# A macaron S4 layer on one core: Newton steps moved to VectorE, the S4 tables cut into pieces, the first weight tile copied on chip, and VectorE's instructions kept in program order

## The chip, the core and the metric

The kernel runs on one core of a Trainium2 chip. The core has a matrix engine (TensorE, "PE" in the profile), three engines for element-wise work (VectorE "DVE", ScalarE "ACT", GpSimd "POOL"), and SyncE ("SP"), which here only starts DMA transfers. The engines run side by side and wait for each other with semaphores. Each engine takes its own instructions in the order in which the program was built. The metric is the time of one execution on the device in microseconds (us), as the median of several runs.

## The reference

The input is 2 x 1024 tokens of 1024 numbers. It goes through a gated feed-forward block with 4-bit weights, then an S4 convolution, then the same feed-forward block again, each with a layer norm before it and a residual around it:

```python
def _dequant(qweight, scales, qzeros, g_idx):
    # W[k,n] = scales[g_idx[k],n] * (w4[k,n] - (z4[g_idx[k],n]+1))
...
xf = x.reshape(-1, x.shape[-1])
h = jax.nn.silu(xf @ Wg) * (xf @ Wu)
out = h @ Wd
...
x = x + 0.5 * _L0_ffn_ref(_layernorm(x, axis=-1), ...)
x = x + _L0_attn_ref(_layernorm(x, axis=-1), ...)
x = x + 0.5 * _L0_ffn_ref(_layernorm(x, axis=-1), ...)
```

`Wg` and `Wu` are 1024 x 2752, `Wd` is 2752 x 1024. Scales and zero points are given for groups of 128 rows, so there are 8 groups for gate and up and 21 for down. The S4 kernel is built from 64 complex poles at 1024 roots of unity, turned into a time response by an inverse DFT, and applied to each channel as a causal convolution, which the kernel does as a product with a Toeplitz matrix.

## The kernel before

**Jobs.** The 2048 tokens are four blocks of 512. `JOBS` (L1046) lists eight feed-forward passes: block 0 and block 1 for the first block of the layer, then both for the second, then the same for blocks 2 and 3. In the text they are job 0 to job 7. Each job is `gate_up` (L485) and then `down` (L548).

**gate_up.** The output columns are 21.5 gate columns and 21.5 up columns of 128 ("units"; even units are gate, odd units are up). They are done in eight waves: five of six units, two of four, one of five. A wave is eight steps, one for each weight group, so a job has 64 steps. In a step every unit gets two matmuls of 128 x 512 (the low and the high part of the split input, `xTl` and `xTh`), accumulated in a PSUM bank of its own. After each step but the last the bank is multiplied by the ratio of two scales (`scaled`, L478), so that one bank can sum over groups. Even units are multiplied on ScalarE (L481) and odd units on VectorE (L483); in job 0 one odd unit of each step goes to ScalarE as well. A unit's next matmul waits for its multiplication. At the end of a wave `gated` (L523) takes Silu on ScalarE (L525), the product `hf` on VectorE (L528), and a split into `hh` and `hl` on GpSimd (L530, L532). There are six accumulator banks, two `hf` buffers and six weight buffers (pool `w`).

**down.** 2 x 22 steps of four banks each, scaled in the same way, with weights `wd`. `back` (L580) turns the result and adds it to the residual on VectorE (L587).

**Weights.** In job 0 the 4-bit weights are unpacked: `split` (L395) makes bytes of nibbles, `dequantize` (L400) subtracts zero points (`q`, L404, on VectorE, into a `w` buffer) and writes the tile to DRAM (L406), from where `load_w` (L462) reads it, three steps ahead. Eight `q` tiles make one wave; `first_weights` (L445) places them 12 to 5 steps ahead of their wave. `down` has the same with `qd` (L434).

**Layer norm.** `moments` (L129) runs eight `bn_stats` and four `bn_aggr` and a first guess of the inverse root on VectorE. `deviations` (L150) refines it by three Newton steps of four tiny instructions each on GpSimd (L156 to L159). `normalized` (L163) applies it on VectorE, `turn` (L188) transposes on TensorE and splits into `xTh` (ScalarE) and `xTl` (VectorE). A call stands at one step of the loop: for a job whose predecessor was a first pass, `moments` at steps 4 and 27 (49 in job 1); for a coming first pass, at step 44 (job 0: at the start of `down`).

**S4 tables.** `s4_poles`, `s4_roots`, `s4_response` and `s4_toeplitz` run once, in job 1 at steps 6, 11, 16 and 20. The largest single instruction is a reciprocal of 128 x 1024 (L652). The convolutions of block 0 follow at steps 34 to 46 of job 1.

**Order.** The loops call hooks in program order, but a scheduler orders the instructions of each engine while the program is built, from its own idea of when inputs are ready, so an instruction can be placed ahead of one that was written earlier. The two calls that concern the first tile are

```python
    first = [normalized_on_act(0, t) for t in range(NT)]
    for i in range(8):
        dequantize(0, i)
    for t in range(NT):
        turn(0, t, first[t], 0, acc)
    for t in range(NT):
        turn(0, t, first[t], 1)
```

and before them `warm()` (L199) has 32 transposes of an identity that nothing reads. `in_order` (L317, job 2, step 30) checks on VectorE that group indices and scales are such that the fast path holds.

Of the kernel before, what the change touches and what calls it, by code (L numbers as in the profile page):

```python
# [20 lines left out]
P = 128  # L21
# [28 lines left out]
def macaron_s4_kernel(  # L50
# [31 lines left out]
    nc = tc.nc  # L82
    u = u.flatten_outer_dims()
# [45 lines left out]
    def moments(b, k, first=0, count=NT):  # L129

        ts = range(first, first + count)
        name = f"{b}_{k}_{first}"
        stats = small.tile([P, NT, 2, 6], F32, tag="stats", name=f"stats_{name}")
        mv = small.tile([P, NT, 2], F32, tag="mv", name=f"mv_{name}")
        for t in ts:
            for i in range(2):
                nc.vector.bn_stats(stats[:, t, i, :], x[b][t][:, bass.ts(i, 512)])  # L137
            nc.vector.bn_aggr(mv[:, t, :], stats[:, t, :, :].rearrange("p a s -> p (a s)"))
        own = slice(first, first + count)
        ve = small.tile([P, NT], F32, tag="ve", name=f"ve_{name}")[:, own]  # L140
        nc.vector.tensor_scalar(ve, mv[:, own, 1], EPS, None, ALU.add)
        r = small.tile([P, NT], F32, tag="r", name=f"r_{name}")
        half = small.tile([P, NT], I32, tag="half", name=f"half_{name}")[:, own]
        nc.vector.tensor_scalar(half, ve.bitcast(I32), 1, None, ALU.logical_shift_right)
        nc.vector.tensor_scalar(  # L145
            r[:, own].bitcast(I32), half, -1.0, float(0x5F3759DF), ALU.mult, ALU.add
        )
        ln[b, first] = (mv, ve, r, own)

    def deviations(b, k, first=0, eng=None):  # L150

        eng = eng or nc.gpsimd
        mv, ve, r, own = ln.pop((b, first))
        e = small.tile([P, NT], F32, tag="e", name=f"e_{b}_{k}_{first}")[:, own]
        for _ in range(3):
            eng.tensor_tensor(e, r[:, own], r[:, own], ALU.mult)  # L156
            eng.tensor_tensor(e, e, ve, ALU.mult)
            eng.tensor_scalar(e, e, -0.5, 1.5, ALU.mult, ALU.add)
            eng.tensor_tensor(r[:, own], r[:, own], e, ALU.mult)  # L159
        for t in range(own.start, own.stop):  # L160
            ln[b, t] = (mv[:, t, 0:1], r[:, t : t + 1], k)

    def normalized(b, t):  # L163
# [3 lines left out]
        return n  # L167

    def normalized_on_act(b, t):
        m, r, k = ln[b, t]  # L170
        n = t4(f"xn_{b}_{k}_{t}")
        less = small.tile([P, 1], F32, tag=f"less{t}", name=f"less_{t}")
        nc.gpsimd.tensor_scalar(less, m, -1.0, None, ALU.mult)
        nc.scalar.activation(n, x[b][t], AF.Identity, bias=less)
        nc.scalar.activation(n, n, AF.Copy, scale=r)  # L175
        return n
# [21 lines left out]

    def warm():  # L199

        ps = bank("warm")
        for _ in range(32):
            nc.tensor.transpose(ps[:, :P], ident, ident)
# [53 lines left out]
    def scales(part):  # L257


        lo = HID * part  # L260
        n = min(HID, WIDE * P - lo)
        row = t4(f"srow_{part}")
        for m, src in enumerate((gate_s, up_s)):
            nc.scalar.dma_start(row[m * GK : (m + 1) * GK, :n], src[:, lo : lo + n])
        ps = bank(f"ps_s{part}")
        u0, u1 = 16 * part, 16 * part + 2 * (n // P)
        for k in range(n // P):
# [3 lines left out]
        if u1 == UNITS - 1:  # L271
            row = t2("srow_half")
            for m, src in enumerate((gate_s, up_s)):
                nc.scalar.dma_start(row[:GK, m * HALF : (m + 1) * HALF], src[:, WIDE * P :])
            nc.tensor.transpose(ps[:, bass.ts(2 * (n // P), GK)], row[:GK, :P], ident[:GK, :GK])
# [4 lines left out]
        inv = t2(f"inv_{part}")[:, : (u1 - u0) * GK]  # L280
        inverse(inv, flat(s), part)
# [35 lines left out]
    def in_order():  # L317

        nc.gpsimd.memset(ok, 1.0)
        nc.sync.dma_start(row_t, c_row)  # L320
        nc.sync.dma_start(shift_t, c_shift)
        in_range(s_gu.rearrange("p u g -> p (u g)"), 0)
        in_range(s_dn.rearrange("p c g -> p (c g)"), 2)
        raw = t4("ix").bitcast(I32)[:32, : 3 * P].rearrange("p (i k) -> p i k", i=3)
# [44 lines left out]

    packed = {}  # L370
# [9 lines left out]
    def fetch_zeros(w):  # L380
        z = t4(f"z_{w}").bitcast(BF16)[:, : width_of(w)]
# [859 lines left out]
```

## Time and profile before

| | us |
|---|---|
| median of 3 runs | 2231.79 |
| lowest and highest run | 2229.93, 2232.19 |
| the profiled execution, as timed | 2234.3 |
| its span in the profile | 2232.5 |
| first matmul of job 0 starts at | 35.8 |
| first matmul of job 1 starts at | 321.2 |
| first matmul of job 2 starts at | 634.8 |
| last transposes start at | 2219.3 |

The profile names an instruction by its line, its engine, its output and inputs, and gives busy time and the mean duration of one. "Idle before" is the time that the engine stood still just before an instruction, with what ended it. Matmuls are pipelined: the profile gives each of the 128 x 512 kind 0.39 us, but they start every 0.23 us. The row PEclk is the clock that TensorE was granted, as a share of the full one. A table of windows gives, for each stretch of the span, the busy time and the number of instructions of each engine.

### The profile page before, as it was taken

To read this page: it belongs to the slowest core of one execution; us is meant where nothing else is said; L and a number is where in the kernel's file an instruction comes from. 1 tells how busy PE (TensorE), PEld (TensorE's weight loads), DVE (VectorE), ACT (ScalarE), POOL (GpSimd) and SP (SyncE) were. 2 spreads that over 40 slices of the span, in tenths; PEclk is the share of its full clock that TensorE was granted. 3 is DMA by queue.
4 is the path that set the end of the run, shared out by engine and by line. 5 is a ranking of instruction groups with operands and counts; after the bars stand their busy time and mean duration, and the time that the engine had idled before them with its cause. 6 is when DMAs were issued, how large, how long until landed. Compare 5 with 4: busy or idle time off the path is not lost.

```text
span 2232.5 us, 28079 instructions
## 1 busy us (share of the span) xinstructions
PE 2152.1 (96%) x9396; PEld 1696.8 (76%) x9396; DVE 1693.7 (76%) x2653; ACT 1455.9 (65%) x2235; POOL 361.5 (16%) x496
## 2 busy tenths in 40 slices
PE   5998999999999999999999999999999999999998
PEld 4776677766887777888788878777788777888876
DVE  6887878666786878777877777867778677777776
ACT  4887775535764576677767777646776467767765
POOL 1232003212011230022102220102201023012210
PEclk7999998999999999999999999999999999999999
DMA  6888864324443545744456444435444355564444
GB/s 237 280 280 270 256 216 126 122 86 152 136 147 107 177 137 165 226 144 134 144 174 193 132 137 136 145 107 156 138 136 147 108 176 137 155 188 143 136 134 129
DMA packets 163526, 359.93 MB, mean 161 GB/s; under 512 B 22268, under 2 KB 27429, under 8 KB 163375
## 3 DMA queue, kind: packets, MB, share of 16 engines
q1 hardware_dynamic: 162746, 357.71, 52.2%
q8 instruction: 78, 1.28, 0.2%
q14 instruction: 74, 0.60, 0.1%
q10 hardware_dynamic: 628, 0.34, 0.1%
HBM read 307.25 MB, written 50.73 MB: 160 GB/s over the span
## 4 chain that ended last, share of the span: by engine, by line
PE 53%; issue 31%; POOL 6%; DVE 5%; DMA 3%; ACT 0%; SPq 0%; POOLq 0%; DVEq 0%; ACTq 0%
PE pg L505 28%; PE po L564 18%; PE pc L810 5%; POOL hl L532 3%; POOL hh L530 2%; DVE pg L483 1%; DMA w<-wq 1%; DMA wd<-wdq 1%; PE pt L182 1%; PE pb L585 1%; DVE po L483 1%; PE st L182 1%; DMA wdq<-qd 0%; DVE q L404 0%; DVE hf L528 0%
## 5 line engine op out<-in xcount | busy, mean ns | idle before, releaser
L481 ACT ACTIVATE pg<-pg,rat 128x512 f32<-128x512 f32 x1264 | 825.4, 662 | 475.5 <-PE pg L505 471.9
L505 PE MATMUL pg<-xTl,w 128*128 128x512 f32 x2752 | 1092.5, 398 | 27.0 <-DVE pg L483 16.3
L505 PE MATMUL pg<-xTh,w 128*128 128x512 f32 x2752 | 1077.6, 393 | 0.0
L483 DVE TENSOR_TENSOR pg<-pg,rat 128x512 f32<-128x512 f32 x1144 | 781.5, 696 | 175.7 <-PE pg L505 166.7
L505 PEld LDWEIGHTS pg<-xTl,w 128*128 128x128 f32 x2752 | 521.6, 190 | 163.9 <-DVE pg L483 29.7
L505 PEld LDWEIGHTS pg<-xTh,w 128*128 128x128 f32 x2752 | 522.2, 190 | 104.8 <-issue 0.2
L564 PE MATMUL po<-hl,wd 128*128 128x512 f32 x1344 | 538.7, 403 | 15.4 <-DVE po L483 10.1
L481 ACT ACTIVATE po<-po,ratd 128x512 f32<-128x512 f32 x670 | 437.6, 662 | 169.2 <-PE po L564 168.7
L564 PE MATMUL po<-hh,wd 128*128 128x512 f32 x1344 | 521.7, 392 | 0.0
L483 DVE TENSOR_TENSOR po<-po,ratd 128x512 f32<-128x512 f32 x610 | 418.7, 697 | 92.9 <-PE po L564 88.7
L564 PEld LDWEIGHTS po<-hl,wd 128*128 128x128 f32 x1344 | 252.2, 188 | 94.8 <-DVE po L483 23.7
L530 POOL CAST hh<-hf 128x512 fp32r<-128x512 f32 x168 | 107.8, 642 | 1243.6 <-DVE hf L528 1197.7
L564 PEld LDWEIGHTS po<-hh,wd 128*128 128x128 f32 x1344 | 253.3, 188 | 45.9
L532 POOL TENSOR_TENSOR hl<-hf,hh 128x512 fp32r<-128x512 f32 x168 | 220.9, 1315 | 13.3
L528 DVE SCALAR_TENSOR_TENSOR hf<-pg,rat,g 128x512 f32<-128x512 f32 x168 | 125.3, 748 | 77.7 <-PE pg L505 29.2
L525 ACT ACTIVATE g<-pg,rat 128x512 f32<-128x512 f32 x168 | 115.8, 689 | 41.4 <-PE pg L505 38.5
L810 PE MATMUL pc<-toeplitz,st 128*128 128x512 f32 (+3 forms) x384 | 126.5, 486 | 0.0
L810 PEld LDWEIGHTS pc<-toeplitz,st 128*128 128x128 f32 x384 | 70.3, 190 | 57.3 <-issue 46.0
L156 POOL TENSOR_TENSOR e<-r 128x4 f32<-128x4 f32 x36 | 9.7, 268 | 498.6 <-DVE r L145 496.6
L818 DVE TENSOR_TENSOR x<-x,pc 128x512 f32<-128x512 f32 x32 | 22.0, 687 | 77.6 <-PE pc L810 77.2
L137 DVE BATCH_NORM_STATS2 stats<-x 128x6 f32<-128x512 f32 x96 | 64.8, 680 | 1.4 <-DMA x<-in_L_attn_u_dram 0.2
L182 PE MATMUL pt<-ident,xn 128*128 128x128 f32 x256 | 42.6, 285 | 16.0 <-ACT xn L175 14.1
(136 smaller groups left out, 674.3 us busy)
## 6 DMA issues: line engine op xcount, KB each, us to landing
w<-wq SPq DMA_DIRECT2D x320, 384.0 KB
wd<-wdq SPq DMA_DIRECT2D x336, 256.0 KB
w<-wq SPq DMA_DIRECT2D x128, 256.0 KB
w<-wq SPq DMA_DIRECT2D x64, 320.0 KB
x<-in_L_attn_u_dram SPq DMA_DIRECT2D x32, 512.0 KB
wq<-q SPq DMA_DIRECT2D x40, 384.0 KB
wdq<-qd SPq DMA_DIRECT2D x32, 256.0 KB
xs<-x SPq DMA_DIRECT2D x16, 512.0 KB
```

The lines of the kernel that those rows point to most:

```text
L137: nc.vector.bn_stats(stats[:, t, i, :], x[b][t][:, bass.ts(i, 512)])
L182: nc.tensor.transpose(ps[:, bass.ts(k, P)], n[:, bass.ts(4 * half + k, P)], ident)
L481: nc.scalar.activation(dst, src, AF.Copy, scale=sc)
L483: nc.vector.tensor_tensor(dst, src, sc.to_broadcast([P, TB]), ALU.mult)
L505: nc.tensor.matmul(p, w[:, bass.ts(col, P)], part[:, g, :], start=(g == 0 and k == 0), stop=(g == GK - 1 and k == 1), skip_group_check=True,)
L525: nc.scalar.activation(g, pg, AF.Silu, scale=rat[:, 2 * f, GK - 1 :])
L528: nc.vector.scalar_tensor_tensor(hf, pu, last, g, ALU.mult, ALU.mult)
L530: nc.gpsimd.tensor_copy(hi, hf)
L532: nc.gpsimd.tensor_tensor(lo, hf, hi.bitcast(F32), ALU.subtract)
L564: nc.tensor.matmul(ps[c], w[:, bass.ts(c, P)], part, start=(f == 0 and k == 0), stop=(f == NF - 1), skip_group_check=True,)
L585: nc.tensor.transpose(ps[:, bass.ts(c, P)], yT[a, c][:, bass.ts(t, P)], ident)
L810: nc.tensor.matmul(ps[:, lo - 512 * nh :], lhsT(c), toeplitz[:, lo - P * c : end - P * c], start=(c == 0), stop=(c == last),)
```

## The change

Newton's steps move to VectorE with three instructions each instead of four, and one more that scales the result (constants 3, 12 and 768 and the factor 1/8192 carry the halving). `moments` and `deviations` lose their partial forms. At the start, ScalarE takes the mean off while the moments of the next tile run, the first tile of weights is copied from the `q` buffers into the weight buffer by eight DMAs that ScalarE issues, and the second half of the first block is turned in steps 0 to 3 instead of before step 0. The scales are read in four pieces at steps 2, 12, 20 and 28 instead of three and one (before the loop, 1, 3 and 12), from SyncE's queue. The `q` tiles of wave 1 stand at steps 1 to 4. One of the odd units that ScalarE took in job 0 goes back to VectorE in every fourth step. The S4 functions become one generator, advanced once a step from step 2 of job 1; the reciprocal is cut in eight and two multiplications go to ScalarE; the layer norm, turning and convolution of block 0 in job 1 start eight steps later (the convolutions at steps 42 to 54, `moments` after them at 57). `warm()` is gone. Last, every VectorE instruction is made to follow the one written before it, and so is every ScalarE instruction of the part ahead of the jobs.

```diff
+    def in_written_order(*engines):
+        last = {}
+        for ins in list(nc.cur_bb.bb.instructions):
+            if ins.engine in engines:
+                if ins.engine in last:
+                    tc.add_manual_dep(
+                        ins,
+                        last[ins.engine],
...
+                last[ins.engine] = ins.name
...
-    def deviations(b, k, first=0, eng=None):
-        eng = eng or nc.gpsimd
-        mv, ve, r, own = ln.pop((b, first))
-        e = small.tile([P, NT], F32, tag="e", name=f"e_{b}_{k}_{first}")[:, own]
-        for _ in range(3):
-            eng.tensor_tensor(e, r[:, own], r[:, own], ALU.mult)
-            eng.tensor_tensor(e, e, ve, ALU.mult)
-            eng.tensor_scalar(e, e, -0.5, 1.5, ALU.mult, ALU.add)
-            eng.tensor_tensor(r[:, own], r[:, own], e, ALU.mult)
+    def deviations(b, k, sign=1.0):
+        mv, ve, r = ln.pop(b)
+        e = small.tile([P, NT], F32, tag="e", name=f"e_{b}_{k}")
+        for three in (3.0, 12.0, 768.0):
+            nc.vector.tensor_tensor(e, r, r, ALU.mult)
+            nc.vector.tensor_tensor(e, e, ve, ALU.mult)
+            nc.vector.scalar_tensor_tensor(r, e, three, r, ALU.subtract, ALU.mult)
+        nc.vector.tensor_scalar(r, r, -sign / 8192, None, ALU.mult)
...
+    first_tile = wpool.tile([P, width_of(0)], F32R, tag="w", name="w_0_0")
...
         nc.vector.tensor_tensor(q, src, z, ALU.subtract)
         dst = w_q[w].rearrange("(r j) n -> j r n", j=8)[j]
+        if w == 0:
+            nc.scalar.dma_start(first_tile[j:P:8].bitcast(F32), q[: P // 8].bitcast(F32))
         nc.sync.dma_start(dst, q.bitcast(F32))
...
-                s = s0 + j if w > 1 else j // 2
+                s = s0 + j if w > 1 else (1, 2, 2, 3, 3, 3, 4, 4)[j]
                 at(up, s, lambda w=w, j=j: dequantize(w, j))
...
     def load_w(j, s):
+        if j == s == 0:
+            return first_tile
...
-                    on_act = unit % 2 == 0 or (j == 0 and pos == 1)
+                    on_act = unit % 2 == 0 or (j == 0 and pos == 1 and g % 4 < 3)
...
         dr = t4("s4_dr")
-        nc.vector.tensor_scalar(dr, cs, neg[:, 0:1], None, ALU.mult)
+        nc.scalar.activation(dr, cs, AF.Copy, scale=neg[:, 0:1])
         di = sn
-        nc.vector.tensor_scalar(di, sn, alpha, None, ALU.mult)
+        nc.scalar.activation(di, sn, AF.Copy, scale=alpha)
+        yield
...
-        nc.vector.reciprocal(den, den)
+        for c in range(NC):
+            yield
+            nc.vector.reciprocal(den[:, bass.ts(c, P)], den[:, bass.ts(c, P)])
...
+    def s4_tables():
+        yield from s4_poles()
+        yield
+        yield from s4_roots()
+        yield
+        s4_response()
+        yield
+        s4_toeplitz()
...
-                    late = 22 if j == 1 else 0
+                    late = 30 if j == 1 else 0
...
             if j == 0:
-                at(up, 1, lambda: scales(1))
-                at(up, 3, lambda: scales(2))
-                at(up, 12, scales_down)
+                for s, k0, k1 in ((2, 3, 11), (12, 11, 19), (20, 19, WIDE)):
+                    at(up, s, lambda k0=k0, k1=k1: scales(k0, k1, scale_rows(k0, k1)))
+                at(up, 28, scales_down)
+                for t in range(NT):
+                    at(up, t, lambda t=t: turn(0, t, first[t], 1))
...
             if j == 1:
-                for s, f in ((6, s4_poles), (11, s4_roots), (16, s4_response), (20, s4_toeplitz)):
-                    at(up, s, f)
+                tables = s4_tables()
+                for s in range(2, 42):
+                    at(up, s, lambda: next(tables, None))
...
-    warm()
-    scales(0)
-    split(0)
     fetch_zeros(0)
-    moments(0, 1)
-    deviations(0, 1)
-    first = [normalized_on_act(0, t) for t in range(NT)]
+    srow = scale_rows(0, 3, nc.scalar)
+    first = []
+    def less_mean(t, m):
+        n = t4(f"xn_0_1_{t}")
+        nc.scalar.activation(n, x[0][t], AF.Identity, bias=m, scale=-1.0)
+        first.append(n)
+        if t == 1:
+            split(0)
+    moments(0, 1, less_mean)
+    deviations(0, 1, -1.0)
     for i in range(8):
         dequantize(0, i)
-    for t in range(NT):
-        turn(0, t, first[t], 0, acc)
-    for t in range(NT):
-        turn(0, t, first[t], 1)
+    scales(0, 3, srow)
+    for t in range(NT + 1):
+        if t < NT:
+            nc.scalar.activation(first[t], first[t], AF.Copy, scale=ln[0, t][1])
+        if t:
+            turn(0, t - 1, first[t - 1], 0, acc)
+    in_written_order(mybir.EngineType.Activation)
     x.pop(0)
     fast()
+    in_written_order(mybir.EngineType.DVE)
```

The rest of the diff places the `yield`s of the S4 functions (29 pieces are used of 40 steps), moves the small index and shift loads into `in_order`, puts the zero points into smaller buffers, and drops the turned input of a job at its end rather than at its start.

## The prediction

> **What bounds the kernel now.** I read the page first, then a table of windows, one for each job, then the order of time in three places: the start, the large reciprocal of job 1, and a call of `moments` in job 2.
>
> ```profile
> PE 2152.1 (96%) x9396; PEld 1696.8 (76%) x9396; DVE 1693.7 (76%) x2653; ACT 1455.9 (65%) x2235; POOL 361.5 (16%) x496
> ...
> PEclk7999998999999999999999999999999999999999
> ```
>
> TensorE is busy for 96% of the span, and the granted clock dips only at the start and in one slice of job 1. So a change gains only where TensorE idles, and loses wherever it makes TensorE idle.
>
> ```profile
> 35.80:321.20 285.40, 264.28 (x1104) 200.95 (x1103) 233.55 (x388) 218.37 (x354) 49.18 (x54) 0.97 0.81 262
> 321.20:634.80 313.60, 303.54 (x1278) 234.16 (x1276) 229.76 (x375) 177.00 (x272) 49.78 (x69) 0.96 0.43 129
> 634.80:919.90 285.10, 280.97 (x1228) 218.51 (x1226) 220.57 (x357) 176.01 (x270) 46.98 (x79) 1.00 0.48 146
> ...
> 1413.20:1695.20 282.00, 279.15 (x1225) 218.92 (x1224) 209.65 (x325) 176.19 (x270) 43.81 (x66) 1.00 0.46 137
> ...
> 1977.20:2219.30 242.10, 240.65 (x1065) 195.77 (x1064) 184.03 (x267) 170.26 (x259) 39.14 (x42) 1.00 0.49 144
> ```
>
> Each line is a job (0, 1, 2, 5, 7): its stretch and length, then the busy time and count of PE, PEld, DVE, ACT and POOL, then the clock and the DMA share. Job 7 has no convolution, job 5 does: their 242.1 and 282.0 us are what undisturbed jobs take, with under 3 us of PE idle each. Only jobs 0 and 1 hold anything to win. Job 0 takes 285.4 against about 242: its waves start 23 to 24 us apart where eight steps of twelve matmuls at the 0.229 us pitch would take 22, and DMA is busy for 81%. Job 1 takes 313.6 against 282.0: an excess of 31.6.
>
> The excess of job 1 shows in the timeline (start, duration, engine, line; in brackets the idle time before and what ended it):
>
> ```profile
> 346.79 6.54 DVE L652 RECIPROCAL s_cos<-s_cos 128x1024 f32<-128x1024 f32 x1
> ...
> 351.48 0.50 PE L505 MATMUL pg<-xTl,w 128*128 128x512 f32 x1 [0.75 <-ACT pg L481]
> ...
> 353.95 0.80 PE L505 MATMUL pg<-xTl,w 128*128 128x512 f32 x1 [1.74 <-DVE hf L528]
> ...
> 354.54 0.63 PE L505 MATMUL pg<-xTh,w 128*128 128x512 f32 x1
> ```
>
> While VectorE is held for 6.54 us, one even unit goes on through ScalarE, a pair of matmuls every 1.48 us; then TensorE waits for `hf`, and its next matmuls take 0.63 us instead of 0.39. At other times VectorE's extra work is cheap, because it is dealt out:
>
> ```profile
> 640.20 2.10 DVE L483 TENSOR_TENSOR pg<-pg,rat 128x512 f32<-128x512 f32 x3
> ...
> 643.57 0.20 DVE L138 BATCH_NORM_AGGREGATE mv<-stats 128x2 f32<-128x12 f32 x1
> 643.69 0.64 DVE L137 BATCH_NORM_STATS2 stats<-x 128x6 f32<-128x512 f32 x1
> 644.24 1.28 DVE L483 TENSOR_TENSOR pg<-pg,rat 128x512 f32<-128x512 f32 x2
> ```
>
> One or two instructions of `moments` stand between scalings (L483): the scheduler interleaved them, and TensorE shows no gap there.
>
> **What the Trainium skill says.** "TensorE: Matmul & The Clock Gate", section "Architectural detail", has VectorE and ScalarE as strict first-in-first-out queues: an instruction cannot pass the one ahead of it. The stall at L652 agrees. The same page, "What's actually happening", has the clock fall to half after an idle window of about 3.4 us; the trace agrees in kind (0.63 against 0.39 us), although TensorE was not idle but thinly used. "VectorE: DVE Perf Modes", section on the TRN2 errata, gives 691 ns for an fp32 two-input operation of 512 elements; the page of this kernel has 696 for L483, but successive ones start 0.60 us apart, and I use 0.60. "DMA: Bandwidth & Descriptors", "Anatomy of one DMA", has about 2 us fixed for a GpSimd-issued transfer; here, issued by SP, writing the zero points took 3.06 us and reading them 2.70.
>
> **The change, part by part** (negative is a gain).
>
> *Start.* The first gate matmul starts at 35.8. ScalarE's L175 waited until 26.56 for twelve Newton instructions of GpSimd (20.07 to 26.5). On VectorE they are ten of some 0.17 us, so the second limit takes over: VectorE's eight `q` tiles, which start at 15.51 with the zero points and end at 24.5, less about 0.6 because scale work moves behind them: 23.9. In the changed order eight DMA issues of ScalarE stand ahead of its multiplications and wait for `q` 0 to 7, so ScalarE starts near 24.3. Then four multiplications at 1.07, five copies at 0.55, and 0.9 to the matmul: 32.2, thus −3.6. Bounds −5.5 (scales leave more room) and −2 (DMA issues cost ScalarE time, of which the page shows none at this place). The second half, turned in steps 0 to 3, puts 4 × 0.6 us on each engine into wave 0.
>
> *Job 0.* Wave 0 took 28.8 us and its VectorE load, with the delayed halves and wave 1's `q` tiles, stays at about that: 0. In waves 1 to 4 eight `q` at 0.87, 24 less 2 scalings at 0.6 plus two given back, three `hf` at 0.67 and the split sum to 22 to 24 against 22 of TensorE, with no freedom of order: +3 (0 to +8). Waves 5 to 7 lasted 18.5, 20.0 and 22.9 against 14.6, 14.6 and 18.3, waiting for weights on the path `q`, write, read; the earlier start and written order shift this by −3 to 0, I take −1.5. The block of `moments` at the start of `down` now delays `qd`, hence `wdq` and `wd`: +4 (1 to 8). With the start: +2 at the end of job 0 (bounds −6 to +10).
>
> *Job 1.* Of 31.6 us the S4 part's own matmuls are 12.8 (3.4, 7 and 2.4 in three functions), so 18.8 can be had. Slicing removes the 6.54 us hold; what is late next is VectorE's sum. The 30 us of S4 work now stand in steps 2 to 30, beside residual additions, the turn and the block of step 4; over steps 0 to 17 I count 62 us of VectorE for 53 of TensorE at the pitch. So about 9 stay lost, and the block at step 57 costs 3: 12 of 18.8, or −7. Bounds: −15 (the two multiplications given to ScalarE and the 24 pieces all fit) and +3.
>
> *`moments` in one piece.* In the changed program eight `bn_stats`, four `bn_aggr` and three tiny instructions stand together, a step's scalings follow, then ten tiny Newton steps. From the block's start to the `hf` that ends the step's wave or the scalings that follow: 5.7 for the block, 9 × 0.6 of scalings, 1.5 Newton, 3 × 0.67 and 1.2 of `hf` waiting for one of its two buffers behind GpSimd: 15.8 us, where 12.1 is normal. TensorE can run ahead only with even units, and the built order indeed puts even units three to five steps ahead around each block. But three even scalings on ScalarE take 3 × 0.62 = 1.86 us, and the six matmuls they feed take 1.37: TensorE is then 74% used, and the banks run out at a wave's end. The loss lies between 26% of 5 us, 1.2, and the whole delay plus half-clock matmuls, 4.5. I take 2.8. Eight such blocks in jobs 2 to 6 (steps 4 and 27 of jobs 2, 5 and 6, step 44 of jobs 3 and 4): +22 (10 to 36). Job 7 has none.
>
> *`in_order`.* Its 7 to 8 us of VectorE work were scattered; now they stand as one piece at step 30 of job 2, three steps behind a block, and a check bit waits for a TensorE result placed behind one even chain: +5 (1 to 9).
>
> *Nothing.* Moving scale DMAs from ScalarE's to SP's queue, smaller zero buffers and the missing `warm` cost nothing: ScalarE's busy share is 65%, and SP only issues. If scale DMAs delay weight issues on SP, which run three steps ahead, job 0's bound covers it. Newton off GpSimd is worth nothing in steady jobs; GpSimd is 16% busy.
>
> Sum: +2 − 7 + 22 + 5 = +22. The profiled execution took 2234.3 us (2.5 above the median, 1.8 above its span); the differences are added to the median, 2231.8: 2254.
>
> **Rivals.** *Main case, 0.48:* as above, 2254, own range 2240 to 2270.
>
> *Other side, hidden blocks, 0.17:* even units run ahead well enough that a block costs at most 0.5 us (eight: 4), `in_order` 1, while job 1 returns 13, the start 4 and job 0 loses 2 after it: 2231.8 + 4 + 1 − 13 − 4 + 2 = 2222, or 2218 if job 0 keeps level. For it: TensorE's built order already allows for the blocks, and 31.6 us are really there in job 1. Against it: with ScalarE alone TensorE reached one pair per 1.48 us in the stretch at 346 to 354. It decides from a block's price below about 1.0 us.
>
> *Convoy, 0.20:* each block sends TensorE into the half clock, as at 354, for some microseconds: 5 to 6 each, 44 in all, in place of 22; with job 0 at +6: 2231.8 + 6 − 7 + 44 + 5 = 2280. For it: the clock 0.96 of job 1. Against it: six chains, not one, are open at a block's start.
>
> *A wash, 0.15:* block price 1.5 (12), job 1 −11, `in_order` +2, job 0 0: 2235. Of this case a third lies within 0.2% (4.5 us, what a measurement tells from no change).
>
> **Numbers.** Slower by over 0.2%: main 0.48, convoy 0.20, two thirds of the wash 0.10: 0.78. Same: 0.05. Faster: 0.17. The predicted time is the main case, 2254. The range of 2220 to 2282 takes in most of the hidden case's and the convoy's estimates and leaves about 2 in 10 outside.
>
> **What would show it.** Right: first gate matmul near 32; job 1 near 307; jobs 2, 5 and 6 longer by 5 to 8 us and jobs 3 and 4 by about 3, with PE waiting for DVE L483 around a run of eight L137; job 7 unchanged at 242. Wrong: jobs 2 to 6 as long as before, which is the hidden case; a PEclk below 0.97 in these jobs, which is the convoy; a start later than 35.8, if the DMAs on ScalarE cost it time; or job 0 lengthened beyond 295, which would move the cause from the blocks to the weights' path.

## The result, and the profile after

The changed kernel takes 2315.61 us (median of 4 runs, 2314.11 to 2320.16), the one before 2230.86 in the same comparison. The ratio is 1.0383, with a 95% interval of 1.0365 to 1.0401. The forecast had the direction right (slower), but 2254 was 62 us too low, and the time lies outside the range of 2220 to 2282. The forecast column below splits the prediction's sum by job.

The page of the changed kernel, busy time of the engines and granted clock:

```profile
PE 2186.8 (95%) x9364; PEld 1677.6 (73%) x9364; DVE 1726.3 (75%) x2792; ACT 1444.0 (62%) x2229; POOL 322.3 (14%) x350
...
PEclk9999999999999999999999999999999999999999
```

VectorE's work grew by only 33 us (1693.7 to 1726.3), and TensorE has as many products to do as before. An average says nothing of where 80 us of span went. The table by job does (jobs 0, 1, 2, 5, 7; stretch, length, then busy time and count of PE, PEld, DVE, ACT, POOL, clock, DMA share, GB/s):

```profile
36.40:363.90 327.50, 283.53 (x1116) 201.81 (x1116) 237.21 (x376) 214.06 (x346) 44.10 (x42) 0.94 0.71 232
363.90:683.00 319.10, 305.68 (x1278) 225.29 (x1276) 236.33 (x435) 176.17 (x274) 40.74 (x45) 0.98 0.41 126
683.00:976.20 293.20, 285.31 (x1228) 218.37 (x1226) 219.68 (x363) 174.79 (x270) 40.19 (x45) 0.99 0.45 138
1478.80:1768.00 289.20, 284.27 (x1226) 218.05 (x1224) 214.62 (x345) 174.56 (x270) 39.48 (x42) 0.99 0.44 133
2057.80:2312.50 254.70, 242.88 (x1081) 197.33 (x1080) 188.03 (x272) 170.88 (x259) 39.14 (x42) 0.99 0.47 145
```

Set against the kernel before, and with the jobs not shown (the gate_up and down parts are told apart by the first matmul of each):

| | before | after | difference | forecast |
|---|---|---|---|---|
| first matmul of job 0 | 35.8 | 36.4 | +0.6 | −3.6 |
| job 0 | 285.4 | 327.5 | +42.1 | +5.6 |
| job 1 | 313.6 | 319.1 | +5.5 | −7 |
| jobs 2 to 6 | 1342.5 | 1374.8 | +32.3 | +27 |
| job 7 to the end | 255.3 | 254.7 | −0.6 | 0 |
| span | 2232.5 | 2312.5 | +80.0 | +22 |

More than half of the loss is in job 0, where the forecast was +5.6. The waves of job 0, measured from one wave's first `hh` on GpSimd to the next (the first from the first matmul), show where:

| wave | 0 | 1 | 2 | 3 | 4 | 5 | 6 | 7 |
|---|---|---|---|---|---|---|---|---|
| before | 28.7 | 24.3 | 23.4 | 22.7 | 23.0 | 18.5 | 20.2 | 22.9 |
| after | 31.4 | 31.5 | 31.7 | 31.8 | 22.0 | 21.3 | 19.2 | 23.5 |

Waves 1, 2 and 3 are 7.2, 8.3 and 9.1 us longer. These are the waves into which the change puts scales (steps 12, 20 and 28; a first small piece is still read before the loop, and step 2 lies in wave 0). Wave 4, which unpacks eight `q` tiles like them and has as many scalings on VectorE (15) but no scales, is no longer than before. The timeline of the changed kernel in wave 1 (start, duration, engine, line; in brackets idle time and what ended it):

```profile
80.64 6.74 ACT L493 ACTIVATE pg<-pg,rat 128x512 f32<-128x512 f32 x11 [0.24 <-PE pg L517]
...
80.95 0.29 SPq L262 DMA_DIRECT2D srow<-in_L_ffn_up_scales_dram  x1
...
88.21 0.66 PE L272 MATMUL ps_s<-ident,srow 16*128 16x16 f32 x8
88.91 0.29 DVE L283 COPY s_gu<-ps_s 128x128 f32<-128x128 f32 x1 [6.71 <-PE ps_s L272]
...
91.15 0.95 DVE L412 TENSOR_TENSOR q<-even,z 128x768 fp32r<-128x768 uint8 x1
92.02 1.29 DVE L495 TENSOR_TENSOR pg<-pg,rat 128x512 f32<-128x512 f32 x2
92.76 0.79 PE L517 MATMUL pg<-xTl,w 128*128 128x512 f32 x1 [3.89 <-DVE pg L495]
```

and the stretch after that wait, in a table of windows:

```profile
92.76:98.50 5.74, 5.74 (x14) 4.35 (x15) 5.64 (x9) 0.82 (x2) 0.00 (x0) 0.50 0.73 258
```

Read the timeline from the bottom. TensorE waits 3.89 us for an odd scaling, and then runs for 5.74 us at a granted clock of 0.50: its matmuls start every 0.43 us there instead of every 0.23. That scaling was written after the copy of the scales, and VectorE stood 6.71 us in front of that copy. The copy waits for eight small transposes on TensorE. Those need the row of scales, which was only asked for at 80.95; and in the built order they stand behind the rest of the wave's even matmuls, which ScalarE feeds at its own pace (eleven scalings in 6.74 us). So each engine waits for the next, and the odd units of the last steps of the wave come one after the other afterwards. VectorE stands 6.71, 6.01 and 5.78 us in this way in waves 1 to 3, and TensorE after it 3.89, 2.07 and 2.92 us.

The start, in the timeline of the changed kernel:

```profile
18.30 10.32 ACTq L415 DMA_DIRECT2D w<-q  x8
...
28.66 2.19 ACT L1201 ACTIVATE xn<-xn,r 128x1024 f32<-128x1024 f32 x2 [9.93 <-DMA w<-q]
...
36.40 0.50 PE L517 MATMUL pg<-xTl,w 128*128 128x512 f32 x1 [1.52 <-DVE xTl L204]
```

Newton's steps do end early (VectorE has `r` at 17.4), but ScalarE spends 18.3 to 28.6 on the eight copies of the first tile and multiplies only then, 2.1 us later than the 26.56 of before.

The S4 reciprocal of job 1 and a call of `moments` in job 3, both from VectorE's timeline:

```profile
406.16 0.94 DVE L675 RECIPROCAL s_cos<-s_cos 128x128 f32<-128x128 f32 x1
...
408.80 0.93 DVE L675 RECIPROCAL s_cos<-s_cos 128x128 f32<-128x128 f32 x1
...
1096.31 0.70 DVE L495 TENSOR_TENSOR pg<-pg,rat 128x512 f32<-128x512 f32 x1 [0.21 <-PE pg L517]
1096.92 1.28 DVE L153 BATCH_NORM_STATS2 stats<-x 128x6 f32<-128x512 f32 x2
...
1102.65 0.17 DVE L158 TENSOR_SCALAR ve<-mv 128x4 f32<-128x4 f32 x1
1102.86 0.17 DVE L161 TENSOR_SCALAR half<-ve 128x4 int32<-128x4 int32 x1
1103.06 0.17 DVE L162 TENSOR_SCALAR r<-half 128x4 int32<-128x4 int32 x1
1103.14 1.29 DVE L495 TENSOR_TENSOR pg<-pg,rat 128x512 f32<-128x512 f32 x2
```

The slicing does what it says: a piece of 0.94 us every 2.6 us in place of 6.54 at once. The moments block also is what was expected: no odd scaling starts between 1096.3 and 1103.1, where they had followed each other within a microsecond.

### The profile page after: what moved, and what is told of

It is laid out like the page before. It is cut to its first block, busy times and chain, and to the rows that moved or that the text cites. A ratio compares the mean times of both kernels' runs of the same rounds, so it can differ in the third digit from the quotient of the medians.

```text
span 2312.5 us, 28066 instructions
## 1 busy us (share of the span) xinstructions
PE 2186.8 (95%) x9364; PEld 1677.6 (73%) x9364; DVE 1726.3 (75%) x2792; ACT 1444.0 (62%) x2229; POOL 322.3 (14%) x350
## 4 chain that ended last, share of the span: by engine, by line
PE 54%; issue 32%; DVE 5%; POOL 4%; DMA 3%; ACT 1%; ACTq 0%; POOLq 0%; DVEq 0%
PE pg L517 35%; PE po L578 13%; PE pc L851 4%; POOL hl L546 2%; POOL hh L544 2%; DMA w<-wq 1%; DVE pg L495 1%; ACT pg L493 1%; DVE stats L153 1%; PE pb L599 1%; DMA wd<-wdq 1%; DVE q L412 1%; DVE hf L542 0%; PE pt L189 0%; PE st L189 0%
## 5 line engine op out<-in xcount | busy, mean ns | idle before, releaser
L493 ACT ACTIVATE pg<-pg,rat 128x512 f32<-128x512 f32 x1256 | 813.6, 662 | 537.8 <-PE pg L517 530.9
L517 PE MATMUL pg<-xTh,w 128*128 128x512 f32 x2752 | 1064.6, 394 | 0.0
L539 ACT ACTIVATE g<-pg,rat 128x512 f32<-128x512 f32 x168 | 114.6, 691 | 44.8 <-PE pg L517 34.7
L204 DVE TENSOR_TENSOR xTl<-pt,xTh 128x512 fp32r<-128x512 f32 x64 | 44.0, 689 | 27.2 <-ACT xTh L203 26.3
L153 DVE BATCH_NORM_STATS2 stats<-x 128x6 f32<-128x512 f32 x96 | 59.7, 664 | 0.0
```

The source lines that it names most:

```text
L204: nc.vector.tensor_tensor(lo, ps, hi.bitcast(F32), ALU.subtract)
L493: nc.scalar.activation(dst, src, AF.Copy, scale=sc)
L517: nc.tensor.matmul(p, w[:, bass.ts(col, P)], part[:, g, :], start=(g == 0 and k == 0), stop=(g == GK - 1 and k == 1), skip_group_check=True,)
L539: nc.scalar.activation(g, pg, AF.Silu, scale=rat[:, 2 * f, GK - 1 :])
```

## The experiments

The first theory (W) is that the written order on VectorE is the cost. Its rival (S) is that the new places and queues of job 0 and of the S4 tables cost as much in any order. The later runs take W apart: which waits, in which jobs, and what the other parts of the change are worth without it. All are single edits of one of the two kernels unless said otherwise. Times of jobs and waves are those of one profiled execution of each kernel. In job 0 two such executions can differ by some 5 us although that job's program is unchanged (shown below with the S4 pieces), so a few us there are not to be read.

### The written order taken away

```diff
     fast()
-    in_written_order(mybir.EngineType.DVE)
     x.clear()
```

> The changed kernel without the last line that keeps VectorE in written order; all else stays. Theory W (the written order is the cost: VectorE stands in order at the scales of job 0, 6.7 + 6.0 + 5.8 us, and the moments stand as one block): job 0 returns to 285 to 295 us, jobs 2, 5 and 6 to 282 to 286, jobs 3 and 4 to 246 to 248, together 2230 to 2245 us. Rival S (the new places of the scales, of the q tiles and of the SyncE queue cost it, whatever the order): job 0 stays above 315 us and the whole at 2270 us or more.

Measured: 2227.56 us, ratio to before 0.9984 (0.9970 to 0.9998). Job 0 took 298.2 us, job 1 300.6, jobs 2, 5 and 6 282.8, 280.6 and 280.6, jobs 3 and 4 246.4 and 245.7. One line of the change is worth 88 us; all the rest together gains about 4 (2231.51 before in the same comparison), hardly more than the noise. Theory W stands in the whole and in jobs 2 to 6, which are even 0 to 2.3 us shorter than before. VectorE's idle time in front of the copies of the scales falls from 18.5 us in waves 1 to 3 to 1.9 in all. Job 0 missed its span of 285 to 295 by 3 us, so some 13 us of its 42 are not the order's, and neither is the late start: the first matmul came at 37.7.

### The written order alone

```diff
     fast()
+    in_written_order(mybir.EngineType.DVE)
     x.clear()
```

(on the kernel before, with the function `in_written_order` added)

> The kernel before with VectorE in written order and nothing else of the change. Theory W: the eight moments blocks of jobs 2 to 6 cost about 4 us each as in the changed kernel (32 us), the reciprocal of job 1 costs as before, and the scales at steps 1 and 3 of job 0 make VectorE wait there: 2275 us or more. Rival S: 2260 us or less, because the written order is harmless with the old places.

Measured: 2301.14 us, ratio 1.0315 (1.0291 to 1.0339). Jobs 2 to 6 took 293.3, 251.6, 250.0, 286.7 and 286.7 us, 25.8 us more than before in all, 17.2 of it in gate_up: 3 us for the single block of jobs 3 and 4, but only 2 for the pair of jobs 5 and 6, where 4 for each block was expected. The whole reached its mark by way of job 0 (+22.4), job 1 (+11.0) and the start. The first matmul came at 42.0. In job 0, waves 0 and 1 took 33.6 and 30.8 us, and waves 2 to 4 24.6, 22.7 and 22.5. Here the scales stand at steps 1, 3 and 12, that is in waves 0 and 1, and exactly these are the long ones. The wait at step 12 is in VectorE's timeline as an idle 4.97 us ahead of the copy `s_dn<-ps_d`. So the long waves follow the scales, and the loss belongs to the order together with their place. In wave 0 it is not this idle time that makes it long, though: there VectorE stands only 0.61 us in front of a copy of scales, and what costs the rest was not found.

### Scales read ahead of their use

```diff
-at(up, s, lambda k0=k0, k1=k1: scales(k0, k1, scale_rows(k0, k1)))
+at(up, max(0, s - 4), lambda k0=k0, k1=k1: rows.update({k0: scale_rows(k0, k1)}))
+at(up, s, lambda k0=k0, k1=k1: scales(k0, k1, rows.pop(k0)))
...
-at(up, 28, scales_down)
+at(up, 24, lambda: rows.update(d=scale_rows_down()))
+at(up, 28, lambda: scales_down(rows.pop('d')))
```

> The changed kernel with the reads of the scales issued four steps ahead of the step that uses them (the transposes and VectorE's part stay at steps 2, 12, 20, 28). Theory W with the scales as the main term in job 0: VectorE no longer stands 6 us in front of each, waves 1 to 3 fall from 31.6 us to 24 to 27 each, and the whole by 15 to 25 us to 2290 to 2300 us. Rival Q (waves 1 to 3 are long because q tiles, scalings and hf fill VectorE in written order): at most 6 us less, 2309 us or more.

Measured: 2302.04 us, ratio 1.0328 (1.0298 to 1.0358), 13.6 us less than the changed kernel; the expected range began at 15. Waves 1 to 3 fell to 29.0, 27.7 and 26.0, from 31.5, 31.7 and 31.8; only the last is within the 24 to 27 expected. The timeline of this kernel shows VectorE at the same copy (L288 here):

```profile
79.60 1.89 DVE L505 TENSOR_TENSOR pg<-pg,rat 128x512 f32<-128x512 f32 x3
81.40 0.28 DVE L288 COPY s_gu<-ps_s 128x128 f32<-128x128 f32 x1
81.71 0.29 DVE L254 TENSOR_TENSOR sq<-s_gu 128x128 f32<-128x128 f32 x1
...
89.12 1.38 DVE L505 TENSOR_TENSOR pg<-pg,rat 128x512 f32<-128x512 f32 x2 [2.47 <-PE pg L527]
```

The idle time in front of the copy is gone, at all three places. About 12 us of the three waves remain against before. The kernel without written order has 9.4 of them too (26.9, 27.1 and 25.8 us), so most of that remainder is not the order's. The moved scale work (2.24 us from 88.91 to 91.15 above) falls into a stretch (waves 1 to 4) where VectorE is busy for 83% of the time (86.74 of 104.8 us), and is a likely part. In waves 1 to 3 of this kernel TensorE waits 3.2 us for weights (`w<-wq`), 2.2 for `hf` and 2.0 for odd scalings, against 0, 1.7 and 0.5 before. The odd scaling given back to VectorE is hardly a part: it is one in each wave, wave 4 has it too, and wave 4 is no longer than before. How the remainder divides was not shown.

### Moments in twelve parts

```diff
-at(up, 4, lambda: moments(pb, 2))
-at(up, 5, lambda: deviations(pb, 2))
+parts_2 = in_parts(pb, 2)
+for s in (2, 2, 3, 3, 4, 4, 5, 5, 6, 6, 7, 7):
+    at(up, s, lambda g=parts_2: next(g, None))
```

(the later call in steps 22 to 33, the call at 44 in steps 44 to 55, that of job 0's down in its steps 0 to 3)

> The changed kernel with each moments block and its Newton steps cut into twelve parts, spread over six or twelve steps (over four at the start of the down part of job 0); VectorE stays in written order. If the block in one piece is the cost in jobs 2 to 6: jobs 2, 5 and 6 fall from 293, 289 and 290 us to 282 to 286, jobs 3 and 4 from 252 and 250 to 246 to 248, together 25 to 32 us less, 2284 to 2291 us. Rival: the work costs the same wherever it stands in the written order, because VectorE has no room: 2305 us or more.

Measured: 2300.70 us, ratio 1.0314 (1.0291 to 1.0338), 14.9 us less. Neither expectation held: the blocks are a cost, but parts in written order take only about half of the gate_up loss away. The gate_up parts of jobs 3 and 4 fell from 163.6 and 163.5 us to 161.0 and 161.8 (159.9 and 159.8 before), those of jobs 5 and 6 from 200.5 and 201.3 to 198.3 and 198.4 (196.1 and 196.2 before). What did not fall at all are the down parts of jobs 2 to 6: 88.3 to 88.6 us in jobs 2, 3, 5 and 6, where the kernel before has 85.8 to 87.7. That pointed at another wait.

### The half unit later

The end of gate_up and the start of down in the changed kernel (job 3), from VectorE's timeline:

```profile
1141.88 0.76 DVE L556 SCALAR_TENSOR_TENSOR hf_half<-pg,rat,g_half 64x512 f32<-64x512 f32 x1 [1.29 <-POOL hl L546]
1142.67 1.37 DVE L558 CAST hb<-hf_half 64x512 fp32r<-64x512 f32 x1
1144.07 0.69 DVE L559 TENSOR_TENSOR hb<-hf_half,hb 64x512 fp32r<-64x512 f32 x1
1144.79 1.30 DVE L495 TENSOR_TENSOR po<-po,ratd 128x512 f32<-128x512 f32 x2
```

TensorE's timeline at the same place:

```profile
1145.55 0.50 PE L578 MATMUL po<-hl,wd 128*128 128x512 f32 x1 [1.85 <-DVE po L495]
```

VectorE waits 1.29 us for GpSimd's `hl` (the `hf` buffer), does three instructions on the half unit, and the first scalings of down stand behind them. `hb` is read only at the last step of down.

```diff
-                    gated_half(j, ps.pop(unit))
+                    rest.append(gated_half(j, ps.pop(unit)))
...
+            if d == 3:
+                rest.pop()()
```

(`gated_half` now does ScalarE's part and returns the rest as a function)

> The changed kernel, written order kept, with VectorE's three instructions on the half unit (L556, L558, L559) written at step 3 of the down part instead of at the end of gate_up. If the longer down parts (88.6 against 85.9 us in most jobs) come from VectorE standing at L556 for GpSimd's hl while the first scalings of down wait behind it: each down part 1.5 to 2.7 us less, together 9 to 18 us less, 2298 to 2307 us. Rival: down is longer for the work of the layer norm in it, and the whole changes by less than 4 us.

Measured: 2292.71 us, ratio 1.0275 (1.0258 to 1.0292), 22.9 us less, more than expected. The down parts of jobs 2 to 6 are now 84.6 to 84.7 us, shorter than before the change. In this kernel's timeline the scalings come first:

```profile
1135.73 0.70 DVE L495 TENSOR_TENSOR po<-po,ratd 128x512 f32<-128x512 f32 x1 [0.28 <-PE po L587]
1136.64 0.70 DVE L495 TENSOR_TENSOR po<-po,ratd 128x512 f32<-128x512 f32 x1 [0.21 <-PE po L587]
...
1141.47 0.76 DVE L562 SCALAR_TENSOR_TENSOR hf_half<-pg,rat,g_half 64x512 f32<-64x512 f32 x1
```

### The three repairs together

The last three edits in one kernel, written order kept:

```diff
+at(up, max(0, s - 4), lambda k0=k0, k1=k1: rows.update({k0: scale_rows(k0, k1)}))
...
+parts_2 = in_parts(pb, 2)
...
+                    rest.append(gated_half(j, ps.pop(unit)))
```

> The changed kernel, written order kept, with the three repairs together: scales read four steps ahead, moments in twelve parts, the half unit at step 3 of down. One by one they took 13.6, 14.9 and 22.9 us. If they are separate waits in separate places, they add up to 51 us: 2260 to 2270 us, still above the kernel before. Rival (they share one shortage, VectorE's room, so that one takes over where another goes): 2280 us or more.

Measured: 2263.80 us, ratio 1.0145 (1.0128 to 1.0162): 51.8 us less, where the sum of the three is 51.4. That they add up says that they are separate waits in separate places. The kernel stays 1.45% slower than the one before, and almost all of that is job 0. Job 1 is back at 313.9 us (313.6 before) and jobs 2 to 6 together at 1345.4 (1342.5); job 0 takes 313.2 against 285.4, 13.7 us more in gate_up and 14.1 more in down.

### Job 0 in its old places, in written order

```diff
-for s, k0, k1 in ((2, 3, 11), (12, 11, 19), (20, 19, WIDE)):
+for s, k0, k1 in ((1, 3, 11), (3, 11, 19), (5, 19, WIDE)):
...
-                    on_act = unit % 2 == 0 or (j == 0 and pos == 1 and g % 4 < 3)
+                    on_act = unit % 2 == 0 or (j == 0 and pos == 1)
...
-                s = s0 + j if w > 1 else (1, 2, 2, 3, 3, 3, 4, 4)[j]
+                s = s0 + j if w > 1 else j // 2
```

(also: scales read up to four steps ahead, `scales_down` at step 12, the second half turned before step 0, the first tile from DRAM)

> The changed kernel, written order kept, with job 0 in the old places: scales at steps 1, 3, 5 and 12 (read up to four steps ahead), odd unit on ScalarE in every step, q tiles of wave 1 at steps 0 to 3, both halves turned ahead of step 0, first tile from DRAM. Theory P (the new places put VectorE's scale work into waves 1 to 3 where a written order leaves no room): waves 2 and 3 come back to 23 to 25 us from 31.7 and job 0 to 300 to 308 us with the first matmul at 33 to 36; the whole 2285 to 2297 us. Rival O (the order alone makes these waves long, wherever the scales stand): waves 2 and 3 stay at 28 us or more, the whole above 2300 us.

Measured: 2300.99 us, ratio 1.0316 (1.0299 to 1.0332). Waves 2 and 3 came back to 24.5 and 22.1 us as theory P said, so the order alone does not lengthen these waves. But waves 0 and 1 became 37.4 and 28.4, job 0 took 314.4 us, above the 300 to 308 expected, and the whole lies above theory P's 2297. The sum of waves 0 to 3, 112.4 us, is that of the kernel with the scales read ahead (112.9). In written order the old places of job 0, taken together, gain nothing over the new ones with the scales read ahead: the loss only moves to other waves.

### The same places without written order

```diff
     fast()
-    in_written_order(mybir.EngineType.DVE)
     x.clear()
```

(on top of the edits of the run before)

> The changed kernel without the written order on VectorE and with job 0 as before: scales at steps 1, 3, 5 and 12 (read up to four steps ahead), the odd unit on ScalarE in every step, the q tiles of wave 1 at steps 0 to 3, both halves turned ahead of step 0, the first tile from DRAM. If the places of job 0 cost it 6 to 13 us even without the written order: job 0 returns from 298 to 284 to 290 us, the first matmul comes at 33 to 36 us, and the whole falls to 2208 to 2218 us, below both kernels. Rival: job 0 of the changed kernel is bound by its DMA and stays above 295 us, the whole at 2224 us or more.

Measured: 2218.46 us, ratio 0.9947 (0.9930 to 0.9964), below both kernels. Job 0 took 291.1 us, and both this and the whole lie just above the spans expected; waves 0 to 3 sum to 100.8 us, against 105.6 with the new places and 99.1 before.

### The first tile from DRAM

```diff
-        if w == 0:
-            nc.scalar.dma_start(first_tile[j:P:8].bitcast(F32), q[: P // 8].bitcast(F32))
...
-        if j == s == 0:
-            return first_tile
```

> The changed kernel with the first tile of weights read from DRAM as all others, without the eight on-chip copies that ScalarE issues. Theory I (the eight issues, 10.3 us long on ScalarE, hold its multiplications L1201 until 28.7 and so eat the gain at the start): L1201 starts at about 18 to 20 us, and the first gate matmul is then set by the last q tile at about 25, its write and its read, near 31 to 33 us instead of 36.4; the whole 3 to 5 us less. Rival D: the way through DRAM is as long as the issues, first matmul at 35.5 or later and no change of the whole.

Measured: 2314.04 us, ratio 1.0375 (1.0358 to 1.0393), no change against the changed kernel. Half of theory I held: ScalarE multiplies from 19.05, and the first matmul came at 32.8.

```profile
19.05 2.17 ACT L1196 ACTIVATE xn<-xn,r 128x1024 f32<-128x1024 f32 x2
...
32.76 0.77 PE L512 MATMUL pg<-xTl,w 128*128 128x512 f32 x1 [6.38 <-DMA w<-wq]
```

The 3.6 us won here were gone by the end of wave 0, which took 34.7 us instead of 31.4 and ended at the same moment (67.4 against 67.8). In written order something else sets the end of wave 0, so the earlier start bought nothing here; what it is was not found.

### Two parts of the change alone, on the kernel before

S4 tables in pieces (the functions as in the change, nothing else):

```diff
-for s, f in ((6, s4_poles), (11, s4_roots), (16, s4_response), (20, s4_toeplitz)):
-    at(up, s, f)
+tables = s4_tables()
+for s in range(2, 42):
+    at(up, s, lambda: next(tables, None))
...
-late = 22 if j == 1 else 0
+late = 30 if j == 1 else 0
```

> The kernel before with only the S4 tables in pieces from step 2 of job 1, its convolutions eight steps later, and no written order. If the pieces are worth what job 1 showed without the written order (300.6 against 313.6 us): 11 to 14 us less, 2217 to 2221 us. Rival: that gain comes from the other parts of the change, and the pieces alone give at most 4 us.

Measured: 2222.73 us, ratio 0.9964 (0.9950 to 0.9978), 8.7 us less; job 1 fell from 313.6 to 304.2 us. The gain is real, but is less than the 11 to 14 expected. Job 0, which this edit does not touch, took 280.2 us in this profile against 285.4, and its waves 0 to 3 sum to 96.0 against 99.1. That is the spread between single profiles of job 0 spoken of above; the 9.4 us of job 1 are more than that, and the 8.7 of the whole come from several executions.

Newton on VectorE:

```diff
-        eng = eng or nc.gpsimd
+        eng = eng or nc.vector
```

> The kernel before with the Newton steps given to VectorE (the same twelve instructions) and nothing else; no written order. The prediction put this at nothing in steady jobs. Jobs 2, 3, 5 and 6 of the changed kernel without written order were 1.2 to 2.3 us shorter than before. If Newton on VectorE is the cause: those jobs fall by 1 to 2 us each and, with an earlier first matmul by 2 to 4 us, the whole falls to 2218 to 2226 us. Rival: no change in those jobs (within 0.4 us each), the whole 2226 us or more, and the other small parts of the change did it.

Measured: 2219.89 us, ratio 0.9953 (0.9938 to 0.9967), 10.1 us less. Jobs 2, 3, 5 and 6 fell by 3.5, 1.4, 1.5 and 1.6 us; the first matmul came only 1.1 us earlier, where 2 to 4 were expected. It is not worth nothing, and the trace of the kernel before shows why (job 5, from VectorE's and from TensorE's timeline):

```profile
1434.20 0.81 DVE L166 TENSOR_SCALAR xn<-x,mv,r 128x1024 f32<-128x1024 f32 x1 [1.66 <-POOL r L159]
1434.93 1.89 DVE L483 TENSOR_TENSOR pg<-pg,rat 128x512 f32<-128x512 f32 x3
...
1435.68 0.50 PE L505 MATMUL pg<-xTl,w 128*128 128x512 f32 x1 [0.70 <-DVE pg L483]
```

The scheduler placed `normalized` (L166) ahead of three odd scalings. It needs the last of the twelve Newton steps of GpSimd, which take 3.3 us in all (1430.88 to 1434.17, before this line); VectorE stands 1.66 us, and TensorE then waits 0.70 us for a scaling that stood behind. VectorE waits for GpSimd at L166 nine times, 16.4 us in all; in the kernel with Newton on VectorE, never.

### The best version

Job 0 in its old places and no written order, as above, with the half unit later:

```diff
-    in_written_order(mybir.EngineType.DVE)
...
-                    gated_half(j, ps.pop(unit))
+                    rest.append(gated_half(j, ps.pop(unit)))
```

> The version with job 0 as before and no written order (2218 us), and with VectorE's three instructions on the half unit moved to step 3 of the down part. In written order that move took 3 to 4 us from each down part (88.6 to 84.7 us). If the down parts of the free order, at 85.9 us, still hold about 1 us of the same wait: 6 to 12 us less, 2206 to 2213 us. Rival: the scheduler already places these three where they do no harm, 2215 to 2221 us.

Measured: 2209.68 us, ratio to before 0.9901 (0.9886 to 0.9916). The down parts of jobs 2 to 6 fell only by 0.4 to 0.6 us, so the scheduler had indeed dealt with most of that wait. In the profiles the largest single step is in job 0's down part (102.7 to 99.2 us), which is within the spread of that job. Of what the change set out to do, this keeps Newton on VectorE and the S4 pieces, and also the smaller edits at the start. It is the fastest version that was run, not the fastest that the runs suggest: on the kernel before, the pieces alone took 8.7 us and Newton alone 10.1, while the version with both and the old places of job 0 took only 12.9. So something else that it keeps of the change may cost some us; the kernel before with these two parts and the half unit later was not run.

## Why the prediction was wrong

**The step that failed: job 0.** "In waves 1 to 4 eight `q` at 0.87, 24 less 2 scalings [...] sum to 22 to 24 against 22 of TensorE, with no freedom of order: +3 (0 to +8)", and under *Nothing*: "Moving scale DMAs from ScalarE's to SP's queue [...] cost nothing". I counted VectorE's busy time and left the scales out of the waves into which they moved, and their wait altogether. Measured, waves 1 to 3 alone lost 24.6 us, and VectorE stood 18.5 us in front of the scales there. Of the 126.4 us for waves 0 to 3 (after; 99.1 before), 13.5 go when the scales are read ahead (112.9); with the order free instead, 20.8 go (105.6), and 6.5 are left against the kernel before with its old places. That last figure is not much more than the spread of job 0. The count was also too high: it has 24 scalings in a wave, where the trace has VectorE do 15 in each of waves 1 to 4 (14 before), since one odd unit is still ScalarE's in all steps of a wave but one. With 15, the prediction's own durations give about 19 us, by my estimate, and about 21 with the scale work, which is below the 22 of TensorE. So busy time does not account for the loss. In a fixed order the question for each moved instruction is what it waits for, and what stands behind it. Whether SyncE's queue in place of ScalarE's matters was not tried apart.

**The down part of job 0** was put at +4 for the block and measured +14.6. The order is most of it: without it the part took 103.0 us, and on the kernel before the order alone makes it 111.0 from 99.5. But the block is not the place: with the moments cut in parts it stays at 114.9 us. The half unit accounts for 2.3 at most, and all three repairs leave 113.6. In the changed kernel's trace TensorE waits 8.2 us for `wd` loads there (4.0 before), one of them 4.01, and 5.0 us for odd scalings (3.0 before), and in the first 20 us VectorE is busy for 18.4 with the clock at 0.83. Which of VectorE's instructions there stands too early stays open.

**The start** (−3.6, measured +0.6): that the multiplications wait for the copies was seen, and set at the last `q`, 24.3. They began at 28.66, because each issue took ScalarE 0.5 to 1.7 us. The bound named this cost ("DMA issues cost ScalarE time") at 1.6 us and it was 4.4. The run without the copies started at 32.8; that this is near the 32.2 forecast is luck, as its first matmul waits for a weight tile from DRAM (6.38 us) and not for ScalarE, and the whole gained nothing. One reading of the prediction is wrong, though no sum rests on it: the write of the zero points (3.06 us) is issued by ScalarE in the trace (L245), only the read by SyncE.

**Job 1** (−7, measured +5.5): the hold of the reciprocal went, as forecast, and without written order the job took 300.6 us, a gain of 13. In written order 18.5 us of loss took its place, so that even the sign was wrong: 10.2 in gate_up (224.8 us against 214.6) and 8.3 in down (94.3 against 86.0). The prediction had about 9 for VectorE's sum in the first steps and 3 for the block at step 57. With the moments in parts the down part fell to 87.1 and gate_up rose to 227.2, 4.8 us less in all, and with all three repairs the job took 313.9. What the rest of the loss in gate_up is stays open.

**The moments blocks and `in_order`** (+22 and +5 in jobs 2 to 6): the gate_up parts of these jobs are 25.7 us longer in all, and 3.7 us for the single block of jobs 3 and 4, inside the bounds of 1.2 to 4.5. The sum fits, but the mechanism is shown only in part: with the blocks cut up, 13.3 of the 25.7 us went, and jobs 5 and 6 with two blocks each lost 4.4 and 5.1, not twice 3.7. `in_order` was not tried alone. So the good fit of the sum is partly luck. What was missing are the down parts of jobs 2 to 6, +6.6 us against before: the half unit, which moving it later showed.

**Newton on VectorE** was set at nothing in steady jobs on the ground that GpSimd is 16% busy; it is worth about 1.5 us in a steady job and, with jobs 0 and 1, 10 us in all on the kernel before. The share of busy time was the wrong measure: what counted is that VectorE waits in its queue for the end of GpSimd's chain, with scalings behind it. Two waits of TensorE of 0.70 us each come just after such waits in job 5, and both are absent with Newton on VectorE.

**The rivals.** The hidden blocks and the wash are excluded. The convoy (2280) came nearest, for the wrong reason: it put 44 us on the blocks of jobs 2 to 6, where the excess of these jobs is 32 in all, `in_order` included, and the clock 0.99. Two of the prediction's own signs of being wrong came true: a start later than 35.8, from the copies that ScalarE issues, and job 0 beyond 295 us. The second was to point at the weights' path; in waves 1 to 3 it was the scales in a fixed order instead.

## What to carry to other kernels

A fixed order on an engine is not a neutral way to tame a scheduler: every instruction that waits makes all that stand behind it wait, so first list each instruction in that order whose input comes from a transfer or from another engine, and issue that input steps ahead. When work is moved into a stretch that is already full, count its wait and its followers, not only its busy time. An engine that is 16% busy can still be the one that others wait for, so look at what stands behind its last result. And an earlier start is worth something only if nothing else sets the end of the stretch after it.

## What the runs showed of the hardware

The time that an issue holds its engine was not constant. In the changed kernel ScalarE and SyncE each issue a copy of every `q` tile at the start. ScalarE's issues took 0.55 and 0.52 us at first and then 0.93 to 1.74, SyncE's 0.32 to 0.33 and then 0.69 to 1.54. In the run in which SyncE issued alone, each of its eight took 0.32 to 0.33 us. Whether it is the second queue or the form of the on-chip copies that lengthens them was not told apart. ScalarE's arithmetic stood behind its issues: `r` was ready at 17.4, and the multiplication began at 28.66, after the last issue.

After a wait of 3.89 us in wave 1 of job 0, TensorE ran at a granted clock of 0.50 for the next 5.74 us, with matmuls of the 128 x 512 kind every 0.43 us instead of 0.23. So such a wait cost more than its own length.
